# More gather tiles moved from GpSimd to the ScalarE and SyncE queues: 170 and 199 in place of 136 and 109

## The chip, the cores and the metric

The kernel runs on one core of a Trainium2 chip. The metric is device time in microseconds, the median of several executions. A profile of one execution stands beside it. The engines are called PE (TensorE), DVE (VectorE), ACT (ScalarE), POOL (GpSimd) and SP (SyncE).

## The reference

A recommender's attention over a user's features. For 16384 users there are 69 feature ids each and one label id, all rows of a table `emb` of 100001 x 96 floats.

```python
u = emb[batch_user]                       # 16384 x 69 x 96
ql = emb[batch_label[:, 0]]               # 16384 x 96
q = broadcast(ql[:, None, :], u.shape)
z = concatenate([q, u, q - u, q * u], axis=-1)
h = dice(z @ W1 + b1, a1)                 # 64 wide
att = (h @ W2 + b2) @ W3 + b3             # one number per user and feature
pre = where(batch_user < ITEM_NUM, u * att, 0.0)
pooled = einsum('gf,bfe->bge', window, pre)   # ten groups of features
x = concatenate([pooled, ql], axis=-1)
# two more dense layers with dice (200 and 80 wide), then one output per user
```

`dice(x, a) = (a * (1 - p) + p) * x` with `p = sigmoid(x)`. What matters here is `emb[batch_user]`: over a million rows of 384 bytes are fetched from addresses known only at run time.

## The kernel before, in words

The 16384 users form 32 blocks of 512. A block has 69 chunks of 512 (user, feature) rows, and a chunk is four tiles of 128 rows, one row to a partition. Chunks are worked on in pairs, one pair per **step**: 1104 steps, 8832 tiles. A plan written out by hand (`at(step, work)`) gives the program order of all engines.

In each step i the program holds, in this order: attention rows and spreads of earlier pairs (every fourth step, `attend_rows`, `spread`), `hidden(i - 2)`, ACT's row transfers `scalar_rows(i)`, `pool(i - 7)`, and `fetch(i)`. Steps of the dense layers at the top (`top1`, `top2`, `top3`) of an earlier block come after these.

- `fetch(i)` (line 359) brings the eight tiles of a pair. Seven or eight of them come by `gather`, an indirect DMA issued on POOL (line 266), into a buffer `u` of the pool `upool`. PE turns each tile into `ptr` (line 325), and DVE copies it to `uT` (line 376) and multiplies it with the label's row to `quT` (line 379).
- `hidden(i)` (line 389) multiplies with W1 on PE (`ph`), makes dice with two activations on ACT (lines 405 and 406) and a product on DVE (line 407).
- `pool(i)` (line 448) reads the same tiles a second time on PE, seven steps after their fetch, and frees the buffer.

Some tiles do not come by POOL. In chosen chunks the tile in slot 3 (`SLOT`) is fetched **row by row**: 128 DMAs of 384 bytes each, issued by SP for the chunks of `SP_CHUNKS` and by ACT for those of `ACT_CHUNKS`. They land in `ring`, which has `SP_RING` buffers for SP and `ACT_RING` for ACT. The row addresses are offsets held in SBUF; `Singles.load` (line 286) brings a group of them into registers, and `Singles.fetch` (line 301) issues a DMA per row. A tile's rows count up one of eight semaphores per queue; PE waits for it (`wait_for_single`) ahead of that tile's transpose. A queue that refills a ring buffer waits until PE's last read of it. The tiles' offsets are computed once at the start on DVE from ids that one DMA brings.

SP's rows are placed six steps ahead of their pair, a whole tile at a time; SP also loads the ids that POOL's gathers read. ACT's rows are spread over eight steps, 16 in each, between `hidden(i - 2)` and the next activations.

Of the kernel before, what the change touches and what calls it, by code (L numbers as in the profile page):

```python
# [18 lines left out]
P = 128  # L19
# [29 lines left out]

ROW_BYTES = 4 * E  # L50
SLOT = 3
SP_CHUNKS = [2 * (10 * s + 8) + 1 for s in range(109)]
SP_RING = 4
ACT_CHUNKS = [2 * (8 * s + 11) for s in range(136)]
ACT_RING = 3
ACT_ROWS = 16
ACT_STEPS = -(-P // ACT_ROWS)
SINGLES = SP_CHUNKS + ACT_CHUNKS
NSB = (len(SINGLES) + P - 1) // P
NSEM = 8  # L60
# [55 lines left out]
def rec_kernel(  # L116
# [14 lines left out]

    const = ctx.enter_context(tc.tile_pool(name="const", bufs=1))
    ipool = ctx.enter_context(tc.tile_pool(name="ipool", bufs=2))
    upool = ctx.enter_context(tc.tile_pool(name="upool", bufs=14))
    tpool = ctx.enter_context(tc.tile_pool(name="tpool", bufs=4))
    ypool = ctx.enter_context(tc.tile_pool(name="ypool", bufs=6))
    rpool = ctx.enter_context(tc.tile_pool(name="rpool", bufs=2))
# [456 lines left out]
    def at(step, *work):  # L594
        plan.setdefault(step, []).extend(work)

    by_sync = Singles("sp", nc.sync, mybir.EngineType.SP, SP_CHUNKS, 0, range(SP_RING), 32)
    for s, m in enumerate(SP_CHUNKS):
        at(max(0, m // 2 - 6), lambda s=s: by_sync.fetch(s, 0, P))

    by_scalar = Singles(
        "act",
        nc.scalar,
        mybir.EngineType.Activation,
        ACT_CHUNKS,
        len(SP_CHUNKS),
        range(SP_RING, SP_RING + ACT_RING),
        2 * ACT_ROWS,
    )
    turn = {}  # L610
    for s, m in enumerate(ACT_CHUNKS):
        for k in range(ACT_STEPS):
            turn.setdefault(m // 2 - 2 - ACT_STEPS + k, []).append((s, k * ACT_ROWS, min(P, (k + 1) * ACT_ROWS)))

    def scalar_rows(i):

        for s, start, stop in turn.get(i, []):
            by_scalar.fetch(s, start, stop)

    c = NPAIR - CLOSE  # L620
    for i in range(c):
        if i >= 3 and (i - 3) % 4 == 3:
            at(i, rows_of(i - 6, 4))
        if i >= 3:
            at(i, tails_of(i - 3))
        if i >= 4 and (i - 4) % 4 == 3:
            at(i, spread_of(i - 7, 4))
        if i >= 2:
            at(i, hidden_of(i - 2))
        at(i, lambda i=i: scalar_rows(i))  # L630
        if i < c - CLOSE:
            if i >= POOL_LAG:
                at(i, pool_of(i - POOL_LAG))
        else:

            for k in {0: (-15, -14), 1: (-13,), 3: (-12, -11), 4: (-10, -9), 7: (-8, -7)}.get(i - c + 8, ()):
                at(i, pool_of(c + k))
        at(i, fetch_of(i))
# [116 lines left out]
```

## Time and profile before

| | us |
|---|---|
| median of 3 runs | 13618.31 |
| lowest, highest | 13615.05, 13619.52 |
| profiled execution | 10926.71 |
| its span | 10924.9 |

| engine | busy us | share of the span |
|---|---|---|
| PE, matmul | 8862.0 | 81% |
| POOL | 8226.3 | 75% |
| DVE | 4285.5 | 39% |
| ACT | 1897.5 | 17% |

The profiled execution is 0.80 of the median; numbers from the profile are to be read against its own time. Issuing a DMA does not count as busy, so SP has no share and ACT's share does not hold its row transfers. A group's line gives busy time, the mean of one instruction in ns, and the engine's idle time before these instructions with what ended it. A line that begins with ACTq or SPq speaks of the engine's own instruction queue: row transfers, register loads and their waits.

### The profile page before, as it was taken

Reading aid. Unit: us, or ns where it says so; the run is one execution under the profiler, and the core shown is the slowest. Engines: PE = TensorE matmul, PEld = TensorE weight load, DVE = VectorE, ACT = ScalarE, POOL = GpSimd, SP = SyncE. Lnnn points to the kernel's source line nnn. Section 1 sums busy time; section 2 is a strip of 40 time slices with the busy share of each in tenths; the row PEclk is TensorE's granted clock in tenths of the full one; section 3 lists DMA queues with packets and bytes.
Section 4 is the critical chain, followed back from the end, with each engine's and each line's share of the span. In section 5 each row is a group of like instructions: output and inputs, shape, how many; then the busy total and the mean of one; then the engine's idle time right before and its main releaser. Section 6 shows DMA issues by size and latency. Waiting matters only on the chain.

```text
span 10924.9 us, 172203 instructions
## 1 busy us (share of the span) xinstructions
PE 8862.0 (81%) x41797; PEld 4319.5 (40%) x41797; DVE 4285.5 (39%) x7535; ACT 1897.5 (17%) x2761; POOL 8226.3 (75%) x8721
## 2 busy tenths in 40 slices
PE   7878878788887888888878778878888887888878
PEld 3333434343333344333433333334343333433335
DVE  4334333333333333433333333333333333333334
ACT  1111111111111111111111111111111111111112
POOL 7777777777777777777777777777777777777776
PEclk7767777777777777767777777777777777777777
DMA  2212211121111212212111121112212112122111
GB/s 49 42 42 44 42 42 41 42 44 42 42 42 42 44 41 42 42 41 44 42 42 41 42 44 42 42 42 42 44 42 42 42 41 44 42 42 41 42 41 36
DMA packets 344467, 458.51 MB, mean 42 GB/s; under 512 B 202354, under 2 KB 202866, under 8 KB 343330
## 3 DMA queue, kind: packets, MB, share of 16 engines
q0 software_dynamic: 278880, 428.92, 18.7%
q1 hardware_dynamic: 29762, 11.82, 0.5%
q10 hardware_dynamic: 34816, 6.75, 0.4%
q8 instruction: 336, 5.51, 0.2%
q14 instruction: 673, 5.51, 0.2%
HBM read 446.74 MB, written 0.07 MB: 41 GB/s over the span
## 4 chain that ended last, share of the span: by engine, by line
POOL 49%; issue 21%; PE 17%; DMA 12%; DVE 0%; ACT 0%; ACTq 0%; POOLq 0%; DVEq 0%
POOL u L266 48%; DMA u<-in_rows,ids 12%; PE p L502 4%; PE acc L325 4%; PE ph L399 3%; PE ph L403 2%; PE ptr L325 2%; POOL q L266 1%; PE prow L414 1%; PE pa L423 1%; PE ph L396 0%; PE ph L401 0%; PE pc L348 0%; PE patt L431 0%; ACTq L301 0%
## 5 line engine op out<-in xcount | busy, mean ns | idle before, releaser
L266 POOL DMA_INDIRECT u<-in_rows,ids x8587 | 8104.3, 944 | 2620.1 <-issue 2428.2
L325 PE MATMUL ptr<-ident,u 128*96 128x128 f32 x8587 | 2002.8, 332 | 1940.1 <-DMA u<-in_rows,ids 1892.9
L407 DVE TENSOR_TENSOR y<-ph,y 128x512 f32<-128x512 f32 x1104 | 763.5, 692 | 4377.1 <-ACT y L406 4119.6
L325 PEld LDWEIGHTS ptr<-ident,u 128*96 128x96 f32 x8587 | 1139.7, 149 | 2701.4 <-DMA u<-in_rows,ids 2262.6
L325 PEld LDWEIGHTS acc<-rw,u 128*96 128x96 f32 x15930 | 1677.0, 187 | 1204.3 <-issue 977.6
L376 DVE COPY uT<-ptr 96x512 f32<-96x512 f32 x2208 | 1494.1, 677 | 1488.6 <-PE ptr L325 1485.2
L325 PE MATMUL acc<-rw,u 128*96 128x20 f32 x15930 | 1792.5, 258 | 57.8 <-DVE rw L436 41.7
L405 ACT ACTIVATE y<-ph 128x512 f32<-128x512 f32 x1104 | 658.6, 597 | 6308.6 <-PE ph L403 5822.7
L399 PE MATMUL ph<-uT,A 128*64 128x512 f32 x4096 | 1649.8, 883 | 0.0
L403 PE MATMUL ph<-quT,wn 96*64 96x512 f32 x4416 | 1585.2, 788 | 0.0
L379 DVE TENSOR_TENSOR quT<-ptr,qT 96x512 f32<-96x512 f32 x2048 | 1380.2, 674 | 0.0
L406 ACT ACTIVATE y<-y,wn,na1c 128x512 f32<-128x512 f32 x1104 | 898.1, 813 | 36.6
L403 PEld LDWEIGHTS ph<-quT,wn 96*64 96x64 f32 x4416 | 440.7, 188 | 1041.5 <-issue 1040.8
L502 PE MATMUL p<-pooled,wf 96*100 96x512 f32 (+1 forms) x1400 | 693.1, 644 | 0.0
L399 PEld LDWEIGHTS ph<-uT,A 128*64 128x64 f32 x4096 | 264.1, 175 | 616.2 <-issue 608.8
L416 ACT COPY row<-prow 128x512 f32<-128x512 f32 (+1 forms) x277 | 161.6, 583 | 1791.9 <-PE prow L414 1179.1
L470 DVE COPY pooled<-acc 96x160 f32<-96x160 f32 x1008 | 419.9, 417 | 117.6 <-PE acc L325 116.9
L414 PE MATMUL prow<-y,v 128*32 128x512 f32 x2208 | 453.6, 891 | 1.4 <-DVE y L407 1.1
L502 PE MATMUL p<-pre,V 96*100 96x512 f32 (+1 forms) x700 | 394.9, 710 | 3.0 <-DVE x L485 2.7
L502 PEld LDWEIGHTS p<-pooled,wf 96*100 96x100 f32 x1400 | 259.5, 198 | 332.6 <-issue 332.6
L436 DVE SCALAR_TENSOR_TENSOR rw<-patt,bb,wn 128x320 f32<-128x320 f32 x554 | 276.2, 539 | 143.6 <-PE patt L431 142.9
L431 PE MATMUL patt<-ident,row 128*128 128x128 f32 x1108 | 224.9, 340 | 25.1 <-DVE pre L424 22.7
(72 smaller groups left out, 2445.8 us busy)
## 6 DMA issues: line engine op xcount, KB each, us to landing
ring<-in_rows ACTq DMA_DIRECT2D x17408, 0.4 KB
ring<-in_rows SPq DMA_DIRECT2D x13952, 0.4 KB
u<-in_rows,ids POOLq DMA_INDIRECT x8587
ids<-in_idx SPq DMA_DIRECT2D x8, 560.0 KB, 3.9
q<-in_emb,ids POOLq DMA_INDIRECT x128
wf<-in_far SPq DMA_DIRECT2D x1, 1209.0 KB, 6.4
wn<-in_near SPq DMA_DIRECT2D x1, 236.0 KB, 2.8
ids<-in_idx SPq DMA_DIRECT2D x1, 140.0 KB, 2.3
```

Source lines behind the costliest of these rows:

```text
L266: nc.gpsimd.indirect_dma_start(out=dst, out_offset=None, in_=table, in_offset=bass.IndirectOffsetOnAxis(ap=index, axis=0),)
L325: ins = op(out, ring[:, at[0]].bitcast(F32) if at else u[:, 4 * (c % 2) + t, :], other, **how)
L376: nc.vector.tensor_copy(uT[j][0:E], ptr)
L379: nc.vector.tensor_tensor(quT[:, j, :].rearrange("e (s f) -> e s f", f=FM), ptr.rearrange("e (s f) -> e s f", f=FM), by_field(q[:, k * NS ...
L399: nc.tensor.matmul(p, As[n % 2][:, k // 4, :], uT[j], start=True, stop=False)
L403: nc.tensor.matmul(p, Wp, quT[:, j, :], start=False, stop=True)
L405: nc.scalar.activation(y, ph, AF.Sigmoid, scale=S_DICE)
L406: nc.scalar.activation(y, y, AF.Identity, bias=a1c, scale=na1c)
L407: nc.vector.tensor_mul(y, ph, y)
L414: nc.tensor.matmul(pr[32 * k : 32 * (k + 1), :], v2, ys[b + k], start=True, stop=True)
L470: nc.vector.tensor_copy(pooled[n][:, :, k * NS : (k + 2) * NS].rearrange("e g s -> e s g"), pa.rearrange("e j s g -> e (j s) g"),)
L502: nc.tensor.matmul(p1, w[:, h * DH : (h + 1) * DH], x, start=(k == 0), stop=(k == KTOP - 1))
```

## The change

SP's tiles rise from 109 (one per ten steps) to 199 (one per five and a half), with five ring buffers for four. ACT's tiles rise from 136 to 170: its rows become one stream of 20 per step that runs from one tile into the next, for 16 per step in eight steps per tile. Offsets are still loaded 32 at a time; ACT's loads now begin in the middle of a step where the stream crosses a multiple of 32 rows. To make room, `upool` has 13 buffers for 14.

```diff
-SP_CHUNKS = [2 * (10 * s + 8) + 1 for s in range(109)]
-SP_RING = 4
-ACT_CHUNKS = [2 * (8 * s + 11) for s in range(136)]
+SP_CHUNKS = [2 * (int(5.5 * s) + 6) + 1 for s in range(199)]
+SP_RING = 5
+ACT_ROWS = 20
+ACT_CHUNKS = [2 * ((s + 1) * P // ACT_ROWS + 2) for s in range(170)]
 ACT_RING = 3
-ACT_ROWS = 16
-ACT_STEPS = -(-P // ACT_ROWS)
...
-    upool = ctx.enter_context(tc.tile_pool(name="upool", bufs=14))
+    upool = ctx.enter_context(tc.tile_pool(name="upool", bufs=13))
...
-        2 * ACT_ROWS,
+        32,
     )
-    turn = {}
-    for s, m in enumerate(ACT_CHUNKS):
-        for k in range(ACT_STEPS):
-            turn.setdefault(m // 2 - 2 - ACT_STEPS + k, []).append((s, k * ACT_ROWS, min(P, (k + 1) * ACT_ROWS)))
-
     def scalar_rows(i):
 
-        for s, start, stop in turn.get(i, []):
-            by_scalar.fetch(s, start, stop)
+        row, stop = i * ACT_ROWS, min((i + 1) * ACT_ROWS, len(ACT_CHUNKS) * P)
+        while row < stop:
+            s, start = divmod(row, P)
+            n = min(P - start, stop - row)
+            by_scalar.fetch(s, start, start + n)
+            row += n
```

## The prediction

> **What bounds the kernel now.** First the head of the page, for who is busy:
>
> ```profile
> span 10924.9 us, 172203 instructions
> ...
> PE 8862.0 (81%) x41797; PEld 4319.5 (40%) x41797; DVE 4285.5 (39%) x7535; ACT 1897.5 (17%) x2761; POOL 8226.3 (75%) x8721
> ...
> PEclk7767777777777777767777777777777777777777
> ```
>
> By busy share PE would be the bound and POOL second. The groups of instructions correct that:
>
> ```profile
> L266 POOL DMA_INDIRECT u<-in_rows,ids x8587 | 8104.3, 944 | 2620.1 <-issue 2428.2
> L325 PE MATMUL ptr<-ident,u 128*96 128x128 f32 x8587 | 2002.8, 332 | 1940.1 <-DMA u<-in_rows,ids 1892.9
> ```
>
> POOL's idle time is put down to "issue": it waits for nothing. Busy and idle make (8104.3 + 2620.1) / 8587 = 1.249 us from one gather to the next. The 128 gathers of q take (121.3 + 40.7) / 128 = 1.266 us each, so all 8715 fill 10886 us of the 10925 us span. The timeline of POOL shows that it is a metronome:
>
> ```profile
> 5001.98 0.94 POOL L266 DMA_INDIRECT u<-in_rows,ids  x1 [0.30 <-issue]
> 5003.23 0.94 POOL L266 DMA_INDIRECT u<-in_rows,ids  x1 [0.30 <-issue]
> 5004.48 0.95 POOL L266 DMA_INDIRECT u<-in_rows,ids  x1 [0.31 <-issue]
> ```
>
> PE waits for the landed rows (the second group line above), not the reverse. So POOL's count of gathers sets the span, and every tile that SP or ACT fetches instead is worth one pitch of 1.249 us, as long as that tile is not late. What rows cost on those two queues is in the view of line 301 (row transfers) and of line 286 (loads of 32 offsets into registers):
>
> ```profile
> L301 ACTq DMA_DIRECT2D ring<-in_rows x17408: 213/213/530, 18.4 to 10748.1; - x198
> L301 SPq DMA_DIRECT2D ring<-in_rows x13952: 227/228/463, 6.3 to 10459.8; - x200
> ...
> L286 ACTq TENSOR_LOAD <-offsets x544: 2132/2182/2236, 16.1 to 10735.1; - x182
> L286 SPq TENSOR_LOAD <-offsets x436: 2027/2174/2411, 4.1 to 10447.1; - x146
> ```
>
> and the waits of the SP queue, with one of its tiles and some of ACT's steps in the timeline:
>
> ```profile
> SPq L301 <- PE ptr L325: 3556.9, 71, 95.2
> SPq L301 <- PE acc L325: 1324.8, 26, 96.8
> ```
>
> ```profile
> 5095.98 49.11 SPq L301 DMA_DIRECT2D ring<-in_rows  x128
> ```
>
> ```profile
> 5027.94 0.81 ACT L406 ACTIVATE y<-y,wn,na1c 128x512 f32<-128x512 f32 x1
> 5028.01 4.99 ACTq L301 DMA_DIRECT2D ring<-in_rows  x16
> ...
> 5038.39 5.61 ACTq L301 DMA_DIRECT2D ring<-in_rows  x16
> ```
>
> SP is idle for (3556.9 + 1324.8) / 109 = 44.8 us per tile, waiting until a ring buffer has been read. A tile takes it 49.1 us, and its first load of offsets 2.2 us before that: 51.3 us. ACT takes 5.0 to 5.6 us for 16 rows, and its rows start 0.07 us after L406 has started, so they run beside that activation.
>
> [...] I therefore use 1.249 us and not 0.944; the trace shows why, since 0.30 us of every pitch lies outside the span. [...] rows of 213 and 228 ns stretch to 530 and 463 at most, and ACT's 16 rows vary by 12%. [...] the row queues take 0.5% and 0.4% of the DMA engines, the gathers 18.7%. [...]
>
> **The profiled time and the median.** The profiled execution took 10926.7 us, the median is 13618.3, 1.246 times that, and no view shows why. [...] If POOL alone is slower there, SP and ACT have more room than I reckon. Both keep POOL the bound, so I work out the change against 10926.7 and scale by 1.246. The third case is a rival below.
>
> **The change, part by part.**
>
> *Gathers.* 199 + 170 = 369 tiles come by rows, before 109 + 136 = 245. POOL loses 124 gathers: 124 x 1.249 = 154.9 us, all on the path. Its step falls from 8715 / 1104 x 1.249 = 9.86 us to 8591 / 1104 x 1.249 = 9.72 us.
>
> *SP.* 90 tiles more, 11520 rows and 360 loads. Needed 51.3 us per tile; allowed 5.5 x 9.72 = 53.5 us. Off the path, with 4% of room, where before there was 10 x 9.86 = 98.6 us. The start holds: the first tile is ready 4 + 51 us after the start plus its landing, and is read in step 6, when POOL has issued about 59 gathers (74 us). Five buffers suffice: a tile reuses the buffer of the tile 27.5 steps before, which is read last 7 steps after its transpose, so SP can start about 20 steps ahead and needs 5.3. The eight loads of ids share this queue, 0.37 us of issue each, 50 steps before their block begins: being queued behind one tile costs them 5 steps of 50, nothing.
>
> *ACT.* 20 rows a step for 16, 0.625 loads for 0.5. Rows: 20 x 5.1 / 16 = 6.4 us. Loads: 0.625 x 2.25 = 1.4. Compute: 1897.5 / 1104 = 1.72, less the 0.74 of L406 under which rows run: 1.0. Sum 8.8 us of 9.72, 90%. Taking every row at the dearest, 5.61 / 16 = 0.351, and no overlap: 7.0 + 1.4 + 1.7 = 10.1, above the step. I take 8.8, since most steps show 5.0 and the overlap is seen; both ends go into the range. A late ACT holds back y and then, on DVE, L407 and the copies L376 behind it. Two ph buffers and two ptr buffers let that slip by about a step before PE stalls, and thirteen u buffers against a pool lag of 7 let PE slip about five before POOL does.
>
> *Waits.* PE gets 124 more semaphore waits ahead of a transpose; all of its later work queues behind each. They are already satisfied while SP and ACT keep pace (ACT's last row is issued two steps before its tile is read), and PE has 2063 us of idle time, 1.87 us a step, to hide them in. ACT's wait for its ring buffer falls due at least three steps after that buffer's last read; behind it stand the activations. SP has only rows behind it.
>
> *u buffers 14 to 13.* A u buffer is free after 7 steps plus the step in hand, so 13 still leave about five steps ahead. Cost nothing; POOL's wait for PE was 59.8 us in 10925 and is part of the pitch. Without that cover each lost step would cost 9.7 us.
>
> *Start.* 369 offset rows need three groups of 128, not two: 64 KB more in a transfer whose 128 KB landed in 2.2 us. Between nothing and 2 us, once.
>
> Sum: 10926.7 - 154.9 = 10772 us profiled, -1.42%; times 13618.31 / 10926.7 this is 13425 us.
>
> **The rivals.**
>
> *SP becomes the bound (slower).* Both row queues will be issuing nearly all the time[...]. SP falls behind POOL when 128 rows and four loads of 2.28 exceed 53.5 us, at 0.347 us a row; now it is (51.3 - 9.1) / 128 = 0.330. Then PE waits for every fifth or sixth step's SP tile, and the span is 199 tiles plus some 130 us at both ends. The gain is gone at a tile of 54.3 us (0.353 a row). At 0.36, 55.2 us, it is 11115 profiled, 13853 timed. For: 4% of room is little. Against: ACT is at it half the time already, and SP's median row, 228 ns, is one above its shortest.
>
> *ACT becomes the bound.* At 10.1 us a step the span is 1104 x 10.1 = 11150, 13900 timed; between 9.72 and 9.85 part of the gain is left. Against: it takes the dearest row of those shown for all rows.
>
> *The timed runs are bound by PE (same).* PE's mean clock was 0.745; at 0.5 throughout, its 8862 us would be 13204, near the timed 13618. Then 124 gathers fewer bring nothing: 13618, give or take ten. Against: the profiled execution shows no stretch in which PE ran full.
>
> *The change doesn't do what it says.* The tile lists are constants, all 369 differ (SP takes odd chunks, ACT even ones), and row slot 3 exists in every chunk, so the count of gathers must fall.
>
> **How the numbers follow.** The measurement tells 0.2% (27 us) from no change. Forecast 0.60, at 13400 to 13500. SP the bound 0.15, a fifth of it still within 0.2%; ACT the bound 0.12; PE the bound in timed runs 0.13, half of it within 0.2% and the rest slower by its waits. That makes faster 0.60, same 0.10, slower 0.30. The low end takes a pitch a little dearer than the scaling gives; the high end, 13800, takes in the milder half of the slower cases.
>
> **What would show it.** Right: the L266 group at x8463 with an unchanged pitch of 1.249, span near 10770, SP's wait for PE down to about 2 us a tile but present, ACT's 20 rows in 6.2 to 7 us. Wrong: gaps in POOL's metronome with PE as releaser, waits on PE ahead of transposes from the ring, ACT no longer idle before L405, or a span down by 1.4% with an unmoved median.

## The result, and the profile after

The change measured 16500.9 us (median of 4) against 13616.7 us before: 1.212 times as long, interval 1.210 to 1.214. The forecast was 13425 us, the range ended at 13800. The profiled execution of the change took 16513.6 us, so this time profile and median agree.

One thing has to be said ahead of the rest. The profile of before, from which the prediction reckoned, is of another kind than these timed runs. In the runs that follow, the kernel before takes one of two times and none between: 10926 to 10932 us (on four chips; called **undisturbed** below) or 13616 to 13797 us (on three other chips; **frozen**). None of the seven chips showed both kinds, so it is open whether the chip or the time of the measurement decides; **occasion** below stands for both together. The profile shown ahead was of the first kind, the timed runs of the second. Comparisons below stay within a kind.

From the head of the page after, and its chain of waits:

```profile
PE 8939.9 (54%) x41797; PEld 4604.6 (28%) x41797; DVE 4206.8 (25%) x7535; ACT 1884.0 (11%) x2761; POOL 8113.1 (49%) x8597
...
SPq 62%; issue 36%; PE 1%; ACTq 0%; another core or an unknown queue 0%; DMA 0%; ACT 0%; DVE 0%; POOL 0%
SPq L300 53%; SPq L285 9%; ACTq L300 0%; PE p L501 0%; PE acc L324 0%; PE ptr L324 0%; PE ph L398 0%; DMA ring<-in_rows 0%; PE ph L402 0%; PE patt L430 0%; PE prow L413 0%; ACTq L285 0%; ACT y L404 0%; POOL u L265 0%
```

In the profile of before, the first of these two lines read:

```profile
POOL 49%; issue 21%; PE 17%; DMA 12%; DVE 0%; ACT 0%; ACTq 0%; POOLq 0%; DVEq 0%
```

The chain that ended last was POOL's before; now it is SP's queue alone: its row transfers (line 300, the former 301) and its loads of offsets (285, the former 286). Such a chain is inferred from records of semaphore updates, and frozen traces lack most of these (more on this at the end), but SP's own instructions bear it out: from its first load to its last row, at 16375 us of 16512, SP is never idle for more than 1.5 us. The groups of instructions say the same from the other side:

```profile
L265 POOL DMA_INDIRECT u<-in_rows,ids x8463 | 7991.0, 944 | 8262.0 <-PE ptr L324 2740.7
...
L324 PE MATMUL ptr<-ident,ring 128*96 128x128 f32 x369 | 138.4, 375 | 3874.9 <-DMA ring<-in_rows 3750.0
```

POOL has its 124 gathers fewer, as intended, and one gather is as short as before (944 ns). But its idle time has risen from 2620 to 8262 us, because PE frees the buffers late; and PE waits 3875 us ahead of the 369 transposes that read the ring, that is, for rows. The views of line 300 and of line 285 show what has happened to the rows:

```profile
L300 SPq MOVE ring<-in_rows x25472: 1/29/1467, 6.6 to 16374.7; - x199
L300 SPq DMA_DIRECT2D ring<-in_rows x25472: 1/228/1477, 6.7 to 16374.8; - x199
...
L300 ACTq DMA_DIRECT2D ring<-in_rows x21760: 2/213/1401, 64.1 to 16286.4; - x200
L285 SPq TENSOR_LOAD <-offsets x796: 7/2127/2477, 4.5 to 16348.8; - x199
```

The medians are those of before, 228 and 213 ns. The extremes are not: up to 1477 ns, and down to 1 ns, which is no time for an operation that otherwise takes at least 213. Even the MOVE that goes with each transfer (x25472 of both), 29 or 30 ns without exception in the undisturbed traces of before, e0 to e4, e8, e9 and e11 to e13, reaches 1467. Instructions of both queues start in bursts about 0.7 us apart with their records squeezed together (4488 of SP's starts at line 300 follow the one before by 0.70 to 0.72 us, in the undisturbed trace of the same program a single one): the queues freeze and go on. In between, rows run at their old price, the medians above. The timelines of SP and of ACT show the sum:

```profile
5000.03 400.09 SPq L300 DMA_DIRECT2D ring<-in_rows  x625
```

```profile
5016.07 11.18 ACTq L300 DMA_DIRECT2D ring<-in_rows  x20
```

SP moves 625 rows in 400 us, a tile of 128 in 82 us, where 53.5 was the allowance; ACT's 20 rows, here with a load of offsets among them, take 11.2 us. Over the whole trace the median of 20 rows is 12.0 us with a load and 9.9 without, where the undisturbed trace of the change, below, has 8.9 and 6.3.

### The profile page after: what moved, and what is told of

Same layout as the page of the kernel before. It is cut to its first block, busy times and chain, and to the rows that moved or that the text cites. A ratio compares the mean times of both kernels' runs of the same rounds, so it can differ in the third digit from the quotient of the medians.

```text
span 16511.8 us, 204441 instructions
## 1 busy us (share of the span) xinstructions
PE 8939.9 (54%) x41797; PEld 4604.6 (28%) x41797; DVE 4206.8 (25%) x7535; ACT 1884.0 (11%) x2761; POOL 8113.1 (49%) x8597
## 4 chain that ended last, share of the span: by engine, by line
SPq 62%; issue 36%; PE 1%; ACTq 0%; another core or an unknown queue 0%; DMA 0%; ACT 0%; DVE 0%; POOL 0%
SPq L300 53%; SPq L285 9%; ACTq L300 0%; PE p L501 0%; PE acc L324 0%; PE ptr L324 0%; PE ph L398 0%; DMA ring<-in_rows 0%; PE ph L402 0%; PE patt L430 0%; PE prow L413 0%; ACTq L285 0%; ACT y L404 0%; POOL u L265 0%
## 5 line engine op out<-in xcount | busy, mean ns | idle before, releaser
L265 POOL DMA_INDIRECT u<-in_rows,ids x8463 | 7991.0, 944 | 8262.0 <-PE ptr L324 2740.7
L324 PE MATMUL acc<-rw,u 128*96 128x20 f32 x15702 | 1930.5, 268 | 1216.2 <-issue 446.3
L324 PEld LDWEIGHTS acc<-rw,u 128*96 128x96 f32 x15702 | 1810.3, 200 | 2315.8 <-issue 1219.5
L324 PE MATMUL ptr<-ident,ring 128*96 128x128 f32 x369 | 138.4, 375 | 3874.9 <-DMA ring<-in_rows 3750.0
L324 PE MATMUL ptr<-ident,u 128*96 128x128 f32 x8463 | 1531.7, 331 | 422.5 <-issue 328.9
L402 PE MATMUL ph<-quT,wn 96*64 96x512 f32 x4416 | 1533.2, 741 | 49.6 <-issue 48.5
L324 PEld LDWEIGHTS ptr<-ident,u 128*96 128x96 f32 x8463 | 1196.2, 162 | 575.1 <-issue 487.4
L413 PE MATMUL prow<-y,v 128*32 128x512 f32 x2208 | 697.1, 864 | 871.9 <-issue 414.7
L324 PEld LDWEIGHTS ptr<-ident,ring 128*96 128x96 f32 x369 | 56.7, 154 | 3936.0 <-issue 3494.6
L405 ACT ACTIVATE y<-y,wn,na1c 128x512 f32<-128x512 f32 x1104 | 897.5, 813 | 37.2
```

The source lines that it names most:

```text
L265: nc.gpsimd.indirect_dma_start(out=dst, out_offset=None, in_=table, in_offset=bass.IndirectOffsetOnAxis(ap=index, axis=0),)
L324: ins = op(out, ring[:, at[0]].bitcast(F32) if at else u[:, 4 * (c % 2) + t, :], other, **how)
L402: nc.tensor.matmul(p, Wp, quT[:, j, :], start=False, stop=True)
L405: nc.scalar.activation(y, y, AF.Identity, bias=a1c, scale=na1c)
L413: nc.tensor.matmul(pr[32 * k : 32 * (k + 1), :], v2, ys[b + k], start=True, stop=True)
```

## The experiments

**The kernel before, and the parts.** Four kernels measured together: before unchanged (e0); one tile for each row queue (e1, `range(1)` for 109 and 136); SP's part alone (e2); ACT's part alone (e3). Both parts have 13 u buffers. The last column of the table is POOL's sum: its gathers at 1.249 us each, and the 41 us that before takes besides.

> The kernel before, unchanged, for a trace from the same occasion as the timed runs. Theory A (the two row queues freeze when instructions are issued faster than something shared can take, about 12.4 to 12.6 of the profile's instructions per us in the profile after and in the timed runs before): 13617 us, SP's and ACT's row transfers with stalls on a grid of 0.7 us, as in the profile after. Theory B (only the change's SP tiles are too dear): no stalls, POOL without gaps, and 13617 us would have to come from a dearer gather, 1.56 us. If the kernel has two regimes, 10927 us in one of the executions.

> One row tile on each queue instead of 109 and 136; POOL makes 8958 gathers. Both theories: if POOL's pitch is 1.249 us, 8958 x 1.249 + 41 = 11230 us. Theory A: exactly this, so faster than the 13617 us of before although POOL has 243 gathers more, since about 109000 instructions in 11230 us are 9.7 per us. If instead the timed runs are slow for POOL (pitch 1.56 us): 14000 us.

> Only SP's part of the change (199 tiles, 5 buffers; ACT as before with 136 tiles of 16 rows a step). Theory A: about 195600 instructions at 12.4 per us, 15770 us. Theory B (SP's 5.5 steps are too short whatever ACT does): near the whole change, 16300 to 16500 us, with SP never idle.

> Only ACT's part (170 tiles as a stream of 20 rows a step; SP as before with 109 tiles; 13 u buffers, as the third group of offsets leaves no room for 14). Theory A: about 181000 instructions at 12.4 per us, 14600 us. Theory B: 13617 less 34 gathers, 13570 us.

| kernel | us | ratio to before, interval | gathers x 1.249 + 41 |
|---|---|---|---|
| before | 10926.1 | 1.000, 0.999 to 1.001 | 10926 |
| e1, no rows | 11236.5 | 1.028, 1.025 to 1.031 | 11230 |
| e2, SP's part | 10827.3 | 0.991, 0.988 to 0.994 | 10814 |
| e3, ACT's part | 10886.7 | 0.996, 0.995 to 0.998 | 10884 |

This was an undisturbed occasion. Theory A falls in its general form: e2 issues 195601 instructions in 10834 us, 18 per us, with none of the freezes. Theory B's 16300 us for SP's part don't come either. POOL sets the end in all four, and each part by itself gains what its tiles are worth, to within 14 us.

**The whole change, undisturbed** (e4, no edit).

> The whole change, unchanged, beside the kernel before on this occasion. The prediction's own sum: 8591 gathers x 1.249 + 41 = 10771 us, and each part alone has met such a sum within 15 us. Theory A (something shared by the two queues gives way when both issue): far above either part, 16500 us as first measured, with stalls on a 0.7 us grid in both queues. Theory D (the first measurement's occasion was slow for row transfers, whatever the kernel, since the kernel before took 13617 us there and 10926 us here): 10771 us, no stalls.

10784.5 us, 0.987 of before (0.985 to 0.988): theory D. The prediction's sum was 10772. From its groups, its row transfers, SP's waits, and two steps of ACT in the timeline:

```profile
L265 POOL DMA_INDIRECT u<-in_rows,ids x8463 | 7992.2, 944 | 2582.5 <-issue 2382.7
```

```profile
L300 SPq MOVE ring<-in_rows x25472: 29/29/29, 7.3 to 10509.9; - x199
L300 SPq DMA_DIRECT2D ring<-in_rows x25472: 227/228/514, 7.4 to 10510.0; - x199
...
L300 ACTq DMA_DIRECT2D ring<-in_rows x21760: 213/214/695, 18.5 to 10609.6; - x200
```

```profile
SPq L300 <- PE ptr L324: 210.5, 59, 13.4
SPq L300 <- PE acc L324: 64.9, 12, 10.9
```

```profile
5003.94 9.10 ACTq L300 DMA_DIRECT2D ring<-in_rows  x20
...
5016.29 6.40 ACTq L300 DMA_DIRECT2D ring<-in_rows  x20
```

The same program as the one of 16500 us: POOL without gaps, MOVE at 29 ns throughout, and SP still waiting for PE (275 us, 1.4 us a tile), so it keeps up, barely. What differs is the occasion alone, the chip with it.

**SP's room** (e7, e13): a tile per five steps.

```diff
-SP_CHUNKS = [2 * (int(5.5 * s) + 6) + 1 for s in range(199)]
+SP_CHUNKS = [2 * (5 * s + 6) + 1 for s in range(218)]
 SP_RING = 5
 ACT_ROWS = 20
-ACT_CHUNKS = [2 * ((s + 1) * P // ACT_ROWS + 2) for s in range(170)]
+ACT_CHUNKS = [2 * ((s + 1) * P // ACT_ROWS + 2) for s in range(166)]
```

> The change with a SyncE tile per five steps, 218 of them (ACT 166, so that the offsets still fit three groups). The prediction's point of change: SP needs 51.3 to 51.6 us a tile and would be allowed 5 x 9.70 = 48.5, so SP becomes the bound: 218 x 51.5 + 168 = 11400 us, slower than the kernel before, although POOL makes 15 gathers fewer than in the change. Rival (SP has more room than reckoned, POOL stays the bound): 8448 + 128 gathers, 10750 us.

> A SyncE tile per five steps. Where the kernel before takes 10926 us, the prediction's point of change: 218 tiles x 51.5 + 168 = 11400 us, SP the bound. Where it takes some 13700 us: 17625 us as first measured.

The first fell on a frozen occasion: 17625 us, 1.279 of before (1.273 to 1.285). The second on an undisturbed one: 11366 us, 1.040 (1.037 to 1.043). Its chain of waits:

```profile
SPq 79%; issue 18%; PE 2%; ACTq 1%; DMA 0%; ACT 0%; DVE 0%; POOL 0%; POOLq 0%
```

So the point of change lies where the prediction put it: SP's rows run from 6.7 to 11217.4 us without a pause over 0.8 us, (11217.4 - 6.7) / 218 = 51.4 us a tile, SP the bound. Half a step less per tile turns a gain of 1.3% into a loss of 4.0% with no disturbance at all.

**Dear rows** (e5, e14, e17 on the change, e6 on before). Behind every row transfer:

```diff
+                for _ in range(8):
+                    self.engine.wait_ge(self.sems[k], 0)
```

In the program of e5 these eight calls are four wait instructions per row (101930 on SP, for 25472 rows).

> The whole change, and behind every row transfer four instructions on the same queue that wait for nothing (semaphore waits for a value of 0 or more), to make each row dearer by an estimated 4 x 0.05 to 0.07 us from the gaps around such waits in the trace. Theory E (dear rows on the two queues are all that is needed for the 16500 us first measured): a row takes 0.53 to 0.61 us, SP's tile 77 to 87 us, and SP sets the end, 199 tiles, 15400 to 17400 us. Rival (PE's wait for SP's tile is made up elsewhere, or POOL itself was slow in the first measurement): under 12000 us. Theory A (a shared limit near 12.5 instructions per us on every occasion): 393000 instructions, 31000 us.

> The kernel before with the same four waits behind every row. Theory E: SP's tile of 77 to 87 us still fits its 98.6 us, but ACT needs 16 x 0.52 to 0.60 + 2.1 = 10.4 to 11.7 us a step, above POOL's 9.86: bound by ACT at 11500 to 12900 us, towards the 13617 us of the first measurement, and the ratio of the two kernels near 1.3 the wrong way for the change. Rival (only the change is sensitive): 10926 us.

> The change with four empty waits behind every row, once more. Where the kernel before takes 10926 us (no freezes), this makes rows dear by a known amount on an otherwise undisturbed chip: theory E, SP's tile of 77 to 87 us sets the end at 15400 to 17400 us, so dear rows alone would account for the 16500 first measured. Rival (the dearer rows are absorbed, the 16500 needs something else besides): below 12000. Where the kernel before takes some 13700 us: 25112 us as first measured.

> The change with four empty waits behind every row. Where the kernel before takes 10926 us: theory E (dear rows alone turn the change over), SP's tile sets the end at 15400 to 17400 us; rival (absorbed) below 12000. Where it takes some 13700 us: 25000 us as measured twice.

All fell on frozen occasions: 25112, 24889 and 24893 us for the change (1.82 to 1.83 of before, intervals from 1.81 to 1.83), 19986 us for before (1.45, 1.443 to 1.457). On an undisturbed one this was not measured, so theory E is not shown by it. It does say two things. Theory A's fixed rate is wrong (31000 us expected). And since SP's rows fill the run here too (from 6.6 to 24993.8 us in e5), the 512 waits of a tile cost (25112 - 16501) / 199 = 43 us, 0.085 us each on a frozen occasion (0.082 with e14 or e17).

**One queue alone** (e8, e11, e15: SP's 199 tiles, ACT one; e9: ACT's 170, SP one; e10: no rows).

```diff
-ACT_CHUNKS = [2 * ((s + 1) * P // ACT_ROWS + 2) for s in range(170)]
+ACT_CHUNKS = [2 * ((s + 1) * P // ACT_ROWS + 2) for s in range(1)]
```

In e9 `SP_CHUNKS` has `range(1)` in the same way; e10 is e1 once more.

> The change's 199 SyncE tiles with a single ScalarE tile, so that nearly all rows come from one queue. POOL's sum is 8632 + 128 gathers, 10980 us. On an occasion on which the kernel before takes some 13700 us: theory F (each row queue by itself runs about 1.6 times slower there, whatever the other does) 51.4 x 1.6 x 199 + 130 = 16500 us; theory J (the queues freeze only because both issue) 10980 us. On an occasion on which the kernel before takes 10926 us both say 10980.

> The change's 170 ScalarE tiles with a single SyncE tile. POOL's sum is 8661 + 128 gathers, 11018 us. Where the kernel before takes some 13700 us: theory F 8.8 x 1.6 = 14.1 us a step, 15500 us; theory J 11018 us. Where it takes 10926 us: 11018.

> One row tile on each queue. Theories F and J: 11236 us on every occasion, for POOL's pitch of 1.249 us was the same in the profile after as in the one before. So faster than the kernel before where that takes 13700 us, slower where it takes 10926. Theory G (all engines are slower on some occasions): 11236 x 1.25 = 14000 us there.

> The change's 199 SyncE tiles, one ScalarE tile, once more. Where the kernel before takes some 13700 us: theory F (each row queue by itself is about 1.6 times slower there) 16500 us; theory J (only both queues together freeze) 10981 us as before. Where it takes 10926 us: 10981.

> The change's 199 SyncE tiles, one ScalarE tile. Where the kernel before takes some 13700 us: theory F (each row queue by itself about 1.6 times slower there) 16500 us; theory J (only both queues together freeze) 10981 us. Elsewhere 10981 us.

Undisturbed: e8 10981.2 us, e11 10981.6, e9 11021.3, e10 11226.7, all within 10 us of POOL's sums. Frozen: e15 15554 us, 1.142 of before (1.136 to 1.148). Its chain:

```profile
SPq 62%; issue 35%; PE 2%; another core or an unknown queue 0%; DMA 0%; DVE 0%; ACT 0%; POOL 0%; ACTq 0%
```

Theory J falls: with ACT's rows gone SP still needs 15554 / 199 = 78 us of the run for each tile, against 83 with them. So SP's queue is slow there without ACT's rows; these add about 5 us, if the two occasions are alike. For SP theory F is right in kind, 6% high in size. No run shows ACT's queue alone in that condition, and none a kernel without rows.

**The kernel before where it takes 13600 us** (e12, e16, no edit).

> The kernel before, for a trace where it takes some 13700 us, if this is such an occasion. Theory F: ACT's rows and loads fill its step (16 rows at about 0.6 us, 12.4 us a step), POOL has gaps that PE ends, while SP still waits for PE between tiles. Theory J: freezes only while both queues issue, so SP's tiles that fall into ACT's pauses show 0.32 us a row. Elsewhere: 10926 us, POOL without gaps.

> The kernel before, for a trace where it takes some 13700 us, if this is such an occasion. Theory F (each row queue by itself is slower there): ACT fills its step with 16 rows and becomes the bound, POOL's pitch stays 1.249 us but has gaps that PE ends, SP still waits for PE between tiles. Elsewhere: 10927 us, POOL without gaps.

e12 was undisturbed (10927.8 us); e16 has the time that the prediction started from, 13616.3 us. Its chain, its gathers, and POOL and ACT in the timeline:

```profile
PE 27%; ACTq 27%; issue 26%; another core or an unknown queue 8%; ACT 6%; DVE 4%; POOL 1%; DMA 0%; DVEq 0%; POOLq 0%
ACTq L301 24%; PE acc L325 6%; PE ptr L325 5%; PE ph L399 4%; PE ph L403 4%; PE p L502 3%; ACTq L286 3%; ACT y L405 3%; ACT y L406 2%; PE prow L414 2%; POOL u L266 1%; DVE uT L376 1%; DVE quT L379 1%; DVE y L407 1%
```

```profile
L266 POOL DMA_INDIRECT u<-in_rows,ids x8587 | 8101.2, 943 | 5246.7 <-issue 2154.6
```

```profile
5018.61 0.94 POOL L266 DMA_INDIRECT u<-in_rows,ids  x1 [0.30 <-issue]
5021.65 0.94 POOL L266 DMA_INDIRECT u<-in_rows,ids  x1 [2.10 <-remote]
5022.90 0.94 POOL L266 DMA_INDIRECT u<-in_rows,ids  x1 [0.30 <-issue]
```

```profile
5036.53 8.47 ACTq L301 DMA_DIRECT2D ring<-in_rows  x16
...
5048.90 14.12 ACTq L301 DMA_DIRECT2D ring<-in_rows  x16
```

A gather costs what it always costs and follows the last at 1.249 us, but once a step, where a new buffer is due, POOL stands still for two more microseconds. The chain runs through ACT's queue and PE, not through POOL (1%). ACT's 16 rows take 8.5 and 14.1 us here; over the whole trace the median is 8.86 us without a load of offsets and 10.52 with one before the rows, against 4.93 and 7.45 in the profile of before. With its activations ACT's queue is taken for 10.7 us of a step of 12.3 (87%; 71% in before). Theory F had it fill its step; it doesn't quite.

SP still waits for PE between tiles, but one tile, from the start of its first row to the end of its last, takes 98 us on average, for 49 in the profile of before. That is more than in the trace after (80) and in e15 (75), though SP has the fewest tiles here and before takes nearly the same on all three occasions (13616 to 13626 us). So a row on a frozen occasion has no price that belongs to the queue by itself, as theory F would have it: what else the kernel does counts, and a limit shared by several engines, theory A in a weaker form, isn't excluded.

Nor are the two row queues the only ones that freeze. PE's weight loads for `pool` follow one another without a wait, and they are broken up too:

```profile
514.63 0.72 PEld L325 LDWEIGHTS acc<-rw,u 128*96 128x96 f32 x4 [8.75 <-issue]
516.24 0.24 PEld L325 LDWEIGHTS acc<-rw,u 128*96 128x96 f32 x1 [0.90 <-issue]
519.04 0.23 PEld L325 LDWEIGHTS acc<-rw,u 128*96 128x96 f32 x1 [2.56 <-issue]
```

Where neither such a load nor a matmul beside it has a wait, the next one starts more than 0.4 us later in 204 of 4294 cases in e16 and 54 of 4320 in the trace after, most of them near 0.7, 1.4 or 2.1 us, and never in the profile of before or in e4.

So the 13617 us of before are not POOL's time. ACT's row transfers are the largest line of the chain (24%), PE's instructions together have 27%, and 8% has no known releaser. That rows alone make up the difference to 10926 us is argued, not shown.

## Why the prediction was wrong

*The bound.* Right for the profiled execution, wrong for the timed ones. The step that failed stands under "the profiled time and the median": "Both keep POOL the bound, so I work out the change against 10926.7 and scale by 1.246." It took the ratio for a slowness of all queues alike or of POOL alone, which was an assumption. e16 refutes both, and theory G with them: the gather still takes 943 ns at the same pitch, DVE's group y 691 ns and ACT's L405 597 ns, for 944, 692 and 597 in the profile of before. What had slowed was the issuing of instructions, on the two row queues most of all, on PE to a lesser degree. That possibility turns the change's sign, since the change moves work onto just those queues: SP became the bound, at 82.3 us a tile for the 51.3 reckoned and the 53.5 allowed. A gap of 25% between profile and median that nothing explained was not to be scaled away.

*Gathers.* Right: x8463, pitch unchanged, -1.33% measured undisturbed for -1.42% reckoned.

*SP.* The need of 51.3 us a tile was right undisturbed (51.4 in e13; the wait of 1.4 us a tile in e4 for 2 foretold). Frozen it is 82.3 us (from 6.7 to 16374.8 us for 199 tiles). The rival "SP becomes the bound" named the right bound, and its formula holds: 199 x 82.3 + 130 = 16508 us. Its price was mis-sized: it stopped at 0.36 us a row; the runs showed (82.3 - 9.1) / 128 = 0.57, if the loads are put at their old price of 9.1 us a tile. Nor is it the price of both queues issuing at once. Undisturbed that costs little: ACT's 20 rows take 6.05 us with SP idle (e9) and 6.33 with SP busy (e4), SP's tile 48.8 us with ACT's rows gone (e8) and 49.1 with them (medians). Frozen, e15 shows that it is at most the small part (5 us a tile of the 31 above 51.3, if the frozen occasions of the two runs are alike).

*ACT.* 8.8 us a step held undisturbed (9668 us for 1104 steps in the trace of e4), where it didn't set the end. Frozen, ACT's queue is a large part of what holds up before; in the change SP ends later.

*PE the bound in the timed runs.* Wrong as it was meant: it took a PE clock of 0.5 throughout, which the profile of before has in stretches only (0.50 from 5000 to 5005 us, 1.00 from 5020 to 5025), and e16 has a mean of 0.722, for 0.745 in the profile of before. PE is busy for 67% of e16 and waits in between, though it has its share of the chain.

*Buffers and waits.* 13 u buffers cost nothing that the undisturbed runs show beyond the 14 us by which e4 lies over POOL's sum. PE's waits for row tiles are free only while the rows come in time: none of the waits that e4's view lists, down to 23 us, is one for rows, while e13 has 1902 us of them. Frozen they are the place where the 3875 us are lost.

*What stays open.* Why the queues freeze, and whether the chip or the time decides. Four things are seen. MOVE (up to 1467 ns), register loads (down to 7 ns) and PE's weight loads (54 of 4320 cases in the trace after) are hit like transfers, so it isn't the transfer itself. Nor are the DMA engines slower: SP's DMA queue takes 0.5% of their time in the trace after, 1.0% of a shorter span in e4. The gaps have a grain of 0.7 us. And most semaphore updates are missing from the frozen traces (83748 in the one after, 251596 in e4 for the same program), nearly all of them updates by landed DMAs; there the profile of a single core names "remote" as a releaser (559 times ahead of POOL's gathers in e16). Whether the lost records have to do with the freezes is not shown, since no run here was made without the profiler's records. The number of instructions alone doesn't tell which queue is hit: PE has the most (86151, for SP's 51802 and ACT's 47941 in the change) and is hit least of the three.

## What to carry to other kernels

When the median and the profiled time of one kernel differ by more than the runs do among themselves, the profile is of another condition than the one to be predicted; ask first which engine could have slowed, and whether the change adds work to it. A queue planned at 96% of its allowance has no room for any such condition: here the plan gained 1.3% and, where a row cost 0.57 us for 0.33, lost 21%. Cost a transfer of work both ways, by what the old engine saves and by how much dearer the new one may get before the sign turns.

## What the runs showed of the hardware

The same program ran in two sharply separate conditions that depend on the occasion or the chip: 10784 and 16501 us for the change, 10926 to 10932 and 13616 to 13797 for before. In the slower one the gathers keep their 1.249 us pitch, while SP's and ACT's queues, and now and then PE's, stop again and again in steps of about 0.7 us (4488 of SP's starts in the trace after; PE's weight loads in 204 of 4294 cases in e16), and a tile of rows takes SP 75 to 98 us, depending on the kernel, for 49. Undisturbed, one row of 384 bytes costs SP's queue about 0.33 us of issue (42.2 us for 128) and ACT's 0.32 (6.33 us for 20), a load of 32 offsets 2.2 us (medians of 2174 and 2182 ns in the profile of before); moved this way, a tile of 128 rows costs SP's queue 51.4 us (e13), and saves POOL 1.249 us.
